# Attention values in batches of eight heads, one transpose for the row maxima, and an earlier place for two batches in a hand-ordered two-layer kernel

## The chip, the cores and the metric

The kernel runs on one core of one Trainium2 chip. The metric is the device time of one execution in microseconds. Three runs of the kernel before took 4024.37, 4029.41 and 4029.52 us; the median is 4029.41 us. A core has five engines that run at the same time: TensorE (PE in the profile; its weight loads are PEld), VectorE (DVE), ScalarE (ACT), GpSimd (POOL) and SyncE (SP), which here issues nearly all DMAs.

## What is computed

The input x is [16, 512, 128] in float32: 16 batches of 512 tokens. Two layers follow, and each adds two branches to its input, both fed with the normalised input.

```
xn = layernorm(x)
x  = x + memory(xn) + block(xn)              # layer 0
xn = layernorm(x)
x  = x + double_attention(xn) + routed(xn)   # layer 1
```

- `memory`: a small two-layer network is trained through 8 chunks of 64 tokens, one after the other (the scan), and then read out for all tokens.
- `block`: a convolution over 3 tokens, attention with 16 heads of 8 channels, a layer norm, and 8 experts of width 512 that all see every token (weighted by a softmax gate).
- `double_attention`: causal attention with 16 heads; its output goes through a convolution and serves as the queries of a second causal attention with the same keys and values.
- `routed`: 32 experts, each token uses 8 of them, and each expert takes at most 128 tokens.

## The kernel before

**A look and a pass of values.** Attention for one batch is split in two halves `c` of 8 heads each. Every half needs two passes over its scores. The first pass, `largest`, I call a look: TensorE makes scores of 128 queries against up to 512 keys for two heads at a time (tile `s`, stationary `q`, moving `k`), and VectorE takes the row maxima into `nm`. The maxima are then negated, split in two parts [...] (`mp`), turned by TensorE into rows (`tpm`), copied by ScalarE (`m`), stored to memory (`topd`) and read back into two spare rows of the query operand `q`, so that the second scores come out with the maximum already subtracted. The second pass, `weighted`, makes the scores the other way round (keys on the partitions), ScalarE takes the exponential into `e`, GpSimd clears what lies above the diagonal (`affine_select`, in layer 1 only), and TensorE multiplies `e` with the padded values `vp`: four heads at a time, each in its own strip of 32 columns of the array, into one PSUM tile `pc`. When all keys are done, `pc` is copied to `cs`, turned back (`tpc`) and divided by the sums.

**Widths.** In layer 0 each pass has 16 tiles of 512 columns with two heads each. In layer 1 the causal mask leaves 512, 384, 256 and 128 columns; `widths` gives 4 tiles of 512 and 4 of 384 with two heads, 2 of 256 with four heads and 1 of 128 with eight: 11 tiles. Layer 0 has 32 looks, layer 1 has 64 (16 batches, two attentions `i`, two halves `c`).

**Turns.** The order of TensorE's work is written out by hand. Each stage is a generator, and `Turns.run` lets every live stage take one step per turn, in the order of priority: looks (0), passes of values (1), and others. One step of `largest` or `weighted` is one tile. Locks make looks follow each other (`p1`), passes of values too (`p2`), and give the PSUM tile `pc` to one pass (`ctx`). Four score slots (`free_slots`) and three tiles of values (`free_values`) are shared by all batches. `room` and `hold` ration three shared PSUM tiles (`work`).

**Filling with experts.** `ffn(b)`, the experts of layer 0, fills what TensorE has left: each turn adds `TURN` = 2750 minus the estimated load of the turn's other matmuls to a credit, and a unit of expert work (`phe` and its ReLU, or `pye`) costs 1000. Where no experts run, `fill` adds matmuls whose result is not used.

**Layer 1.** For batch b, `middle(b)` finishes layer 0, normalises and routes (logits `prl`, counts `pct`, tables `ctab`, `totT`, `xw`); `front1(b)` makes queries, keys and values; `tops` is a look with its loads (`rows_in`); `back` is a pass of values; `between(b)` makes the second queries; `last(b)` ends the batch. Batches start 44 turns apart (`TBB`), which is four looks of 11 turns. After the last `middle`, the pool `mid` closes, `mo` opens in its place, and `moe`, the routed experts, runs with gathers and scatters issued by GpSimd; `total` stores the result.

Of the kernel before, what the change touches and what calls it, by code (L numbers as in the profile page):

```python
# [17 lines left out]
P = 128  # L18
# [64 lines left out]
def network(ctx: ExitStack, tc: tile.TileContext, a, out):  # L83
# [16 lines left out]
        n: [dram.tile([NT8, 2, 32, S], F32, name=f"{n}{i}") for i in range(3)]  # L100
        for n in ("rq0", "rk0", "rq1", "rk1", "r2")
    }
    topd = [dram.tile([16, S], F32, name=f"top{i}") for i in range(4)]
    acc_b = acc[0:N, :].rearrange("(b t p) d -> b p t d", t=TB, p=P)
    xw_b = xw.rearrange("(b t p) d -> b p t d", t=TB, p=P)
    ctab_v = ctab.rearrange("(e i) n -> e i n", i=NTILE)
# [27 lines left out]
        return cols[:, k : k + 1]  # L134

    pools, done, locks, clock, newest, cleared, held, read, cell = {}, {}, set(), [0], [None], [None], [0], [0], []

    def mark(*m):
        done[m] = clock[0]
# [118 lines left out]

    def ends(stage, name):
        yield from stage  # L260
        mark(name)

    def idle(n):
        for _ in range(n):
# [103 lines left out]
    def largest(slot, causal):  # L368


        q, k, at = slot
        yield from acquire("p1")
        nm = att.tile([P, TB, 2, NH], F32, tag="nm", bufs=2, name="nm")
        for i, n, per, t in widths(causal):
            qt = TB - 1 - i
            s = pools["ps"].tile([P, 2, 512], F32, tag="p1", bufs=pools["p1"], name="s1")
            sv = s[:, :, 0 : per * n].rearrange("p r (i n) -> p r i n", i=per)
            for u in range(per):
                for r in range(2):
                    rr = slice(64 * r, 64 * r + 64)  # L380
                    mm(sv[:, r, u, :], q[rr, t + u, qt * P : (qt + 1) * P], k[rr, t + u, :n])
            if causal and per == 1:

                for r in range(2):
                    newest[0] = nc.vector.tensor_tensor_reduce(  # L385
                        out=sv[:, r, 0, :], in0=sv[:, r, 0, :], in1=row["caus"][:, S - n :], scale=1.0, scalar=-BIG,
                        op0=ALU.add, op1=ALU.max, accum_out=nm[:, qt, r, t : t + 1],
                    )
            else:
                if causal:  # L390
                    for r in range(2):
                        dg = sv[:, r, :, n - P : n]
                        nc.vector.tensor_tensor(dg, dg, bc(row["caus"][:, S - P :], 1, per), ALU.add)  # L393
                newest[0] = nc.vector.tensor_reduce(nm[:, qt, :, t : t + per], sv, AX.X, ALU.max)  # L394
            yield
        locks.remove("p1")
        mp = att.tile([P, TB, 2, 2, NH], F32, tag="mp", bufs=2, name="mp")
        nc.vector.tensor_scalar(mp[:, :, :, 0, :].bitcast(FR), nm, -1.0, None, ALU.mult)
        nc.vector.scalar_tensor_tensor(
            mp[:, :, :, 1, :].bitcast(FR), nm, -1.0, mp[:, :, :, 0, :], ALU.mult, ALU.subtract  # L400
        )
        yield
        yield from room()
        tp = work("tpm")[0:16, :]
        for t in range(TB):
            nc.tensor.transpose(tp[:, t * P : (t + 1) * P], mp[:, t].rearrange("p r i x -> p (r i x)"), ident)
        m = att.tile([16, S], FR, tag="m", bufs=1, name="m")
        nc.scalar.copy(m, tp)
        nc.sync.dma_start(at, m.bitcast(F32))
        for r in range(2):  # L410
            nc.sync.dma_start(
                q[64 * r + 32 : 64 * r + 34, :, :].bitcast(F32),
                at[8 * r : 8 * r + 8, :].rearrange("(i t) s -> i t s", t=NH),
            )
        yield

    def weighted(slot, vp, c, causal, cn):
# [4 lines left out]
        old, ends = [], []  # L422
        got = []

        def values(heads):
            for kt, n, t, r, e in heads:
                g = 2 * (t % 2) + r
                j = t // 2
                mm(
                    got[0][32 * g : 32 * g + 32, S - n :], vp[:, kt, 4 * g + 2 * c + j, :], e,  # L430
                    start=(kt == 0 and j == 0), stop=(kt == TB - 1 and j == 1),
                )
            if kt == TB - 1 and t == NH - 1:
                cs = att.tile([P, S], F32, tag="cs", bufs=1, name="cs")
                nc.scalar.copy(cs, got[0])  # L435
                locks.remove("ctx")
                ends.append(cs)

        def tail(n):
            if not got and "ctx" not in locks:  # L440
                locks.add("ctx")
                got.append(pools["ps"].tile([P, 512], F32, tag="ctx", bufs=1, name="pc"))
            for _ in range(n):
                if got and len(old) >= 4:
                    locks.add("values")
                    values([old.pop(0) for _ in range(4)])

        for kt, n, per, t in widths(causal):
# [12 lines left out]
            if causal:  # L461
# [14 lines left out]
        cs = ends[0]  # L476
        yield from room()
        held[0] += 1
        tp = turn4(lambda t: cs[:, t * P : (t + 1) * P], "tpc")
# [138 lines left out]
    pools.update(ps=ps, p1=1, p2=1, work=3, e=3, pairs=True)  # L618
# [18 lines left out]

    fresh = [score_slot(att, i, (nc.gpsimd, nc.vector, nc.gpsimd)[i]) for i in range(3)]
    fresh += [padded_values(att, i) for i in range(2)]
    th = const.tile([P, NT, NC], F32, name="th")  # L640
    gates = const.tile([P, 2, NC], F32, name="gates")
    beta = const.tile([P, NC], F32, name="beta")
# [427 lines left out]
    def back(layer, b, i, c):  # L1070
# [5 lines left out]
        yield from weighted(z[i, c], z["vp"], c, layer == 1, z["cn"])  # L1076
        mark("back", layer, b, i, c)

    def post0(b):
        yield from after(("back", 0, b, 0, 0), ("back", 0, b, 0, 1))  # L1080
# [40 lines left out]
    with tc.tile_pool(name="p0", bufs=1) as p0:  # L1121

        turns.stages += [(t, 2, stage) for t, stage in zip((0, 8, 22, 2, 24), fresh)]
        stage = norm0(p0)
        turns.stages.append((0, 3, ends(stage, "norm0")))
        turns.run(until=lambda: ("norm0",) in done)
    with tc.tile_pool(name="scan", bufs=1) as s1:
        turns.stages.append((turns.turn, 3, ends(scan(s1), "scan")))
        turns.run(until=lambda: ("scan",) in done)


# [11 lines left out]
    def middle(mid, b):  # L1143
# [49 lines left out]
        nc.sync.dma_start(ctab_v[:, b * TB : (b + 1) * TB, :], ct)  # L1193
# [11 lines left out]

    def front1(b):
        yield from after(("x2", b))
        got = []
        yield from take(free_values, got)
        z = live[1, b] = {"vp": got[0]}  # L1210
        xT = l1.tile([P, S], F32, tag="st", bufs=2, name="xT")
        nc.sync.dma_start(xT, xt[1, b])
        yield from idle(2)
        for n, order in (("q", (0, 0, 1, 1)), ("k", (0, 1, 0, 1))):
# [3 lines left out]
            z["r" + n] = rowd[f"r{n}1"][b % 3]  # L1218
            yield from split_rows(pj, col(f"b{n}1"), order, z["r" + n])
        mark("rows", 1, b, 0)  # L1220
        yield from project_values(D1("wv"), row["bv1"], xT, z["vp"])
        mark("vals", 1, b)

# [348 lines left out]
```

## Time and profile before

| | before |
|---|---|
| median of three runs | 4029.41 us |
| the profiled execution | 4017.65 us |
| its span, first to last instruction | 4015.9 us |
| mean granted TensorE clock | 0.964 |
| TensorE busy | 3599.7 us (90%) |
| VectorE, ScalarE, GpSimd busy | 2379.9, 2200.3, 1655.0 us |
| instructions | 62757 |
| DMA | 370.56 MB, 92 GB/s on average |

The profile is of one execution. Groups are named by the tile they write and the tiles they read, as in `pc<-e,vp`. `s<-kx,qx` are the scores of a look, `s<-qx,kx` those of a pass of values. An idle stretch of an engine is put down to what ended it: `PE pc <- POOL e` means that TensorE stood before a value matmul until GpSimd had cleared the mask. In a view in order of time, neighbours of the same kind are merged (`x8`); in a view of stretches each row has the busy time of each engine in one stretch.

### The profile page before, as it was taken

What the parts mean: (1) busy time and instruction counts of PE and PEld (TensorE: products, weight loads), DVE (VectorE), ACT (ScalarE), POOL (GpSimd) and SP (SyncE); (2) the same over time, 40 slices, a digit from 0 to 9 for tenths busy, and PEclk for the clock granted to TensorE, in tenths of its full rate; (3) what the DMA queues carried; (4) which work ended last, traced back from release to release, by engine and by line L of the source; (5) the groups of instructions that cost most, each with busy time, mean ns of one, the idle gap of its engine ahead of it and who ended that gap; (6) DMA issues with size and microseconds to landing.
All of it is one profiled execution on the core that took longest, in us unless ns stands there. A gap on an engine that the chain in (4) does not pass through costs nothing.

```text
span 4015.9 us, 62757 instructions
## 1 busy us (share of the span) xinstructions
PE 3599.7 (90%) x22665; PEld 1942.9 (48%) x22665; DVE 2379.9 (59%) x5203; ACT 2200.3 (55%) x3687; POOL 1655.0 (41%) x2560
## 2 busy tenths in 40 slices
PE   5889989898999889999999999999999999998886
PEld 2445444444544444555555555555555555543343
DVE  5665655665565555564666665656666666567652
ACT  1555655565556776665555555555555555553333
POOL 5433553354334454134333433443333344333664
PEclk7999999999999999999999999999999999998898
DMA  4222222222223333333333333334333333333233
GB/s 155 63 62 71 65 65 71 64 62 62 73 77 93 107 97 104 105 92 123 99 115 102 98 100 109 107 82 117 102 111 91 113 111 89 102 105 83 71 86 85
DMA packets 274199, 370.56 MB, mean 92 GB/s; under 512 B 42168, under 2 KB 123232, under 8 KB 273120
## 3 DMA queue, kind: packets, MB, share of 16 engines
q1 hardware_dynamic: 266720, 359.71, 31.1%
q0 software_dynamic: 7168, 6.82, 1.0%
q8 instruction: 180, 2.95, 0.3%
q14 instruction: 131, 1.07, 0.1%
HBM read 236.59 MB, written 133.25 MB: 92 GB/s over the span
## 4 chain that ended last, share of the span: by engine, by line
PE 64%; DVE 14%; POOL 7%; ACT 5%; issue 5%; DMA 4%; SPq 1%; POOLq 0%; ACTq 0%; DVEq 0%
PE s L190 16%; PE phe L190 10%; PE pye L571 10%; PE pc L190 9%; DVE nm L394 7%; DVE s L393 2%; ACT e L459 2%; PE pgr L190 2%; PE tp L242 1%; DVE s L385 1%; POOL e L463 1%; PE fill L197 1%; PE po L190 1%; PE pq L190 1%; DMA xT<-xt 1%
## 5 line engine op out<-in xcount | busy, mean ns | idle before, releaser
L459 ACT ACTIVATE e<-s 128x1024 f32<-128x1024 f32 (+1 forms) x1216 | 1189.1, 978 | 801.7 <-PE s L190 759.4
L394 DVE TENSOR_REDUCE nm<-s 128x2 f32<-128x1024 f32 (+1 forms) x704 | 861.6, 1224 | 632.1 <-PE s L190 624.9
L385 DVE CUSTOM_DVE_ANT_0 s<-s,sb_const 128x512 f32<-128x512 f32 (+1 forms) x1024 | 647.7, 633 | 644.8 <-PE s L190 626.0
L463 POOL TENSOR_SCALAR_AFFINE_SELECT e<-e 128x128 f32<-128x128 f32 (+2 forms) x1408 | 465.1, 362 | 1133.9 <-ACT e L459 1126.8
L190 PE MATMUL s<-kx,qx 64*128 64x512 f32 (+3 forms) x3072 | 622.7, 431 | 203.4 <-DVE nm L394 106.4
L190 PE MATMUL pc<-e,vp 128*32 128x512 f32 (+3 forms) x6144 | 702.4, 508 | 40.7 <-POOL e L463 39.5
L190 PEld LDWEIGHTS s<-kx,qx 64*128 64x128 f32 x3072 | 276.6, 188 | 778.5 <-issue 317.8
L571 PEld LDWEIGHTS pye<-ew,hTe 128*128 128x128 f32 x4096 | 519.4, 194 | 210.8 <-issue 187.8
L571 PE MATMUL pye<-ew,hTe 128*128 128x128 f32 x4096 | 574.6, 285 | 6.7 <-ACT hT L840 6.5
L190 PE MATMUL phe<-x1T,ew 128*128 128x512 f32 x1024 | 558.0, 630 | 10.3 <-DMA x1T<-x1d 3.9
L190 PE MATMUL s<-qx,kx 64*128 64x512 f32 (+3 forms) x3072 | 532.7, 372 | 26.9 <-ACT e L459 25.8
L563 ACT ACTIVATE hTe<-phe,sb_cols 128x512 f32<-128x512 f32 x512 | 352.9, 689 | 303.9 <-PE phe L190 303.7
L190 PEld LDWEIGHTS s<-qx,kx 64*128 64x128 f32 x3072 | 289.9, 189 | 124.6 <-issue 63.4
L579 POOL TENSOR_TENSOR ac<-ac,y 128x512 f32<-128x512 f32 x128 | 164.8, 1287 | 385.8 <-ACT y L578 367.3
L393 DVE TENSOR_TENSOR s<-s,sb_const 128x256 f32<-128x256 f32 (+1 forms) x384 | 199.5, 519 | 179.5 <-PE s L190 166.4
L190 PEld LDWEIGHTS pc<-e,vp 128*32 128x32 f32 x6144 | 134.2, 109 | 247.7 <-issue 148.4
L190 PEld LDWEIGHTS phe<-x1T,ew 128*128 128x128 f32 x1024 | 159.2, 194 | 123.1 <-issue 87.0
L578 ACT ACTIVATE y<-pye,pr 128x128 f32<-128x128 f32 x512 | 147.1, 368 | 41.8 <-PE pye L571 41.1
L385 DVE DVE_READ_ACCUMULATOR2_ANT nm<- 128x1 f32 x1024 | 144.9, 142 | 0.0
L197 PE MATMUL fill<-sb_pb,sb_const 128*128 128x512 f32 (+3 forms) x252 | 124.8, 583 | 10.5 <-DMA zrow<-zero 10.0
L435 ACT COPY cs<-pc 128x512 f32<-128x512 f32 x96 | 56.3, 586 | 58.4 <-PE pc L190 55.7
L203 POOL TENSOR_SCALAR rs_t<-ss 128x4 f32<-128x4 f32 (+1 forms) x56 | 11.0, 197 | 165.8 <-ACT sq L256 164.0
(294 smaller groups left out, 4031.3 us busy)
## 6 DMA issues: line engine op xcount, KB each, us to landing
ew<-in_ew SPq DMA_DIRECT2D x256, 256.0 KB
kx<-rk SPq DMA_DIRECT2D x192, 256.0 KB
qx<-rq SPq DMA_DIRECT2D x128, 256.0 KB
rq<-hi SPq DMA_DIRECT2D x64, 256.0 KB
rq<-lo SPq DMA_DIRECT2D x64, 256.0 KB
rk<-hi SPq DMA_DIRECT2D x64, 256.0 KB
rk<-lo SPq DMA_DIRECT2D x64, 256.0 KB
qx<-r SPq DMA_DIRECT2D x64, 256.0 KB
```

The lines of the kernel that those rows point to most:

```text
L190: nc.tensor.matmul(o, lhsT=lhsT, rhs=rhs, start=start, stop=stop)
L197: nc.tensor.matmul(o[:, 0:n], lhsT=ident, rhs=cell[0][:, 0:n], start=True, stop=True)
L385: newest[0] = nc.vector.tensor_tensor_reduce(out=sv[:, r, 0, :], in0=sv[:, r, 0, :], in1=row["caus"][:, S - n :], scale=1.0, scalar=-BIG, ...
L393: nc.vector.tensor_tensor(dg, dg, bc(row["caus"][:, S - P :], 1, per), ALU.add)
L394: newest[0] = nc.vector.tensor_reduce(nm[:, qt, :, t : t + per], sv, AX.X, ALU.max)
L435: nc.scalar.copy(cs, got[0])
L459: nc.scalar.activation(e[:, :, 0 : per * n], s[:, :, 0 : per * n], AF.Exp, scale=SCALE)
L463: cleared[0] = nc.gpsimd.affine_select(out=ev[:, r, :, 0:P], in_=ev[:, r, :, 0:P], pattern=[[0, per], [1, P]], compare_op=ALU.is_ge, fill= ...
L563: nc.scalar.activation(hs[i], ph, AF.Relu, bias=col("fb", i))
L571: nc.tensor.matmul(pye[0][:, t, :], lhsT=h[:, t * P : (t + 1) * P], rhs=w2[e][:, f, :], start=(f == 0 and t == 0), stop=(f == 3), skip_gro ...
L578: nc.scalar.mul(y[:, t, :], pye[0][:, t, :], pr[:, t, e : e + 1])
L579: nc.gpsimd.tensor_tensor(ac, ac, y, ALU.add)
```

## The change

Five things are changed.

- **Maxima.** `mp` is now a part of one of two tiles of 128 columns, zeroed once at the start. One transpose of the whole tile takes the place of four of 16 columns; the copy `m` is 64x128 in place of 16x512, and `topd` has that shape, so that both DMAs out of it read rows of 128.
- **Values.** In layer 1, while `mid` is open, values wait until 8 heads are there, and two batches of four then run in the same turn. The `e` tiles come in turn from two pools of three tiles (`att`, `mid`); before there was one ring of three. `lent` holds the heads whose `e` lies in `mid`; `moe` starts once it is empty. After that, batches of four return.
- **Drain.** What is left of a pass of values after its last tile is a stage of its own (`summed`, priority 2), started in the next turn; it may run two batches in one turn.
- **Counts.** `middle` makes the counts of its four token tiles with one matmul in place of four; `ctab` and `totT` are written by four DMAs each, where one DMA and one VectorE copy did it.
- **Order.** `middle` and `front1` start 28 turns sooner for batch 2, 6 for batch 3, 12 for batch 15; the first looks of batch 2 are 20 turns sooner, and the last look of batch 13 is 8 turns later. `front1` takes its tile of values after the rows are made, not first.

```diff
-    topd = [dram.tile([16, S], F32, name=f"top{i}") for i in range(4)]
+    topd = [dram.tile([TB * 16, P], F32, name=f"top{i}") for i in range(4)]
...
-        mp = att.tile([P, TB, 2, 2, NH], F32, tag="mp", bufs=2, name="mp")
+        padded = maxima.pop(0)
+        maxima.append(padded)
+        mp = padded[:, 0 : TB * 16].rearrange("p (t r i x) -> p t r i x", t=TB, r=2, i=2)
...
-        tp = work("tpm")[0:16, :]
-        for t in range(TB):
-            nc.tensor.transpose(tp[:, t * P : (t + 1) * P], mp[:, t].rearrange("p r i x -> p (r i x)"), ident)
-        m = att.tile([16, S], FR, tag="m", bufs=1, name="m")
-        nc.scalar.copy(m, tp)
+        tp = work("tpm")
+        nc.tensor.transpose(tp[:, 0:P], padded, ident)
+        m = att.tile([TB * 16, P], FR, tag="m", bufs=1, name="m")
+        nc.scalar.copy(m, tp[0 : TB * 16, 0:P])
         nc.sync.dma_start(at, m.bitcast(F32))
...
-        def tail(n):
+        def tail(least):
...
-            for _ in range(n):
-                if got and len(old) >= 4:
-                    locks.add("values")
+            if got and len(old) >= least:
+                locks.add("values")
+                for _ in range(min(len(old) // 4, 2)):
                     values([old.pop(0) for _ in range(4)])
...
-            while len(old) >= 4 and not got and "ctx" in locks:
+            while len(old) >= pools["heads"] and not got and "ctx" in locks:
...
-            tail(2)
-            e = att.tile([P, 2, 512], F32, tag="e", bufs=pools["e"], name="e")
+            tail(pools["heads"])
+            pool = pools["weights"][i % len(pools["weights"])]
+            e = pool.tile([P, 2, 512], F32, tag="e", bufs=3, name="e")
...
+                    if pool is not att:
+                        lent.add(id(old[-1]))
...
         free_slots.append(slot)
+        turns.stages.append((turns.turn, 2, ends(summed(old, tail, last, c, cnv), name)))
+
+    def summed(old, tail, last, c, cnv):
         while old:
-            tail(1)
+            tail(4)
             yield
...
-        pct = work("pct")[0:EXP1, :]
+        pct = work("pct")[:, 0:P]
+        mm(pct, lr.rearrange("p t e -> p (t e)"), row["tri"])
+        ct = mid.tile([P, P], F32, tag="st", bufs=4, name="ct")
+        nc.scalar.copy(ct, pct)
         for t in range(TB):
-            mm(pct[:, t * P : (t + 1) * P], lr[:, t, :], row["tri"])
-        ct = mid.tile([EXP1, TB, P], F32, tag="st", bufs=4, name="ct")
-        nc.scalar.copy(ct.rearrange("e t n -> e (t n)"), pct)
-        nc.sync.dma_start(ctab_v[:, b * TB : (b + 1) * TB, :], ct)
+            of = ct[EXP1 * t : EXP1 * (t + 1), :]
+            nc.sync.dma_start(ctab_v[:, b * TB + t, :], of)
+            nc.sync.dma_start(totT[:, b * TB + t : b * TB + t + 1], of[:, P - 1 : P])
...
-        nc.vector.tensor_copy(totT[:, b * TB : (b + 1) * TB], ct[:, :, P - 1])
...
+    ahead = {2: 28, 3: 6, 15: 12}
...
         early = 0 if b < B - 1 else 12 if i else 16 + 8 * c
+        if (b, i) == (2, 0):
+            early = 20
+        if (b, i, c) == (B - 3, 1, 1):
+            early = -8
         return t0 + b * TBB + 20 + 66 * i + 11 * c - early
...
-        [(t0 + b * TBB + 14, 4, front1(b)) for b in range(B)]
+        [(t0 + b * TBB + 14 - ahead.get(b, 0), 4, front1(b)) for b in range(B)]
...
-        turns.stages += [(t0 + b * TBB, 4, middle(mid, b)) for b in range(B)]
+        turns.stages += [(t0 + b * TBB - ahead.get(b, 0), 4, middle(mid, b)) for b in range(B)]
+        pools.update(weights=[att, mid], heads=8)
         turns.run(until=lambda: ("xw", B - 1) in done)
+        pools.update(weights=[att], heads=4)
+        turns.run(until=lambda: not lent)
```

More of the change, by code (lines that the diff above doesn't have):

```diff
@@ L136, in network @@
     pools, done, locks, clock, newest, cleared, held, read, cell = {}, {}, set(), [0], [None], [None], [0], [0], []
+    lent = set()
     def mark(*m):
@@ L260, in ends @@
         yield from stage
-        mark(name)
+        mark(*name)
     def idle(n):
@@ L403, in largest, with weighted @@
         yield from room()
-        tp = work("tpm")[0:16, :]
-        for t in range(TB):
-            nc.tensor.transpose(tp[:, t * P : (t + 1) * P], mp[:, t].rearrange("p r i x -> p (r i x)"), ident)
-        m = att.tile([16, S], FR, tag="m", bufs=1, name="m")
-        nc.scalar.copy(m, tp)
+        tp = work("tpm")
+        nc.tensor.transpose(tp[:, 0:P], padded, ident)
+        m = att.tile([TB * 16, P], FR, tag="m", bufs=1, name="m")
+        nc.scalar.copy(m, tp[0 : TB * 16, 0:P])
         nc.sync.dma_start(at, m.bitcast(F32))
+        at = at.rearrange("(a r i t) s -> r i t a s", r=2, i=2, t=NH)
         for r in range(2):
[L411 to L414, printed above, removed]
+            rows = q[64 * r + 32 : 64 * r + 34, :, :].bitcast(F32)
+            nc.sync.dma_start(rows.rearrange("i t (a s) -> i t a s", s=P), at[r])
         yield
-    def weighted(slot, vp, c, causal, cn):
+    def weighted(slot, vp, c, causal, cn, name):
         q, k, _ = slot
@@ L421, in weighted @@
         cnv = cn.rearrange("p t (a c j d) -> p (t a) c j d", c=2, j=2, d=DH)
-        old, ends = [], []
+        old, last = [], []
         got = []
         def values(heads):
-            for kt, n, t, r, e in heads:
+            for head in heads:
+                kt, n, t, r, e = head
+                lent.discard(id(head))
                 g = 2 * (t % 2) + r
@@ L436, in values @@
                 locks.remove("ctx")
-                ends.append(cs)
-        def tail(n):
+                last.append(cs)
+        def tail(least):
             if not got and "ctx" not in locks:
@@ L442, in tail @@
                 got.append(pools["ps"].tile([P, 512], F32, tag="ctx", bufs=1, name="pc"))
-            for _ in range(n):
-                if got and len(old) >= 4:
-                    locks.add("values")
+            if got and len(old) >= least:
+                locks.add("values")
+                for _ in range(min(len(old) // 4, 2)):
                     values([old.pop(0) for _ in range(4)])
-        for kt, n, per, t in widths(causal):
-            while len(old) >= 4 and not got and "ctx" in locks:
+        for i, (kt, n, per, t) in enumerate(widths(causal)):
+            while len(old) >= pools["heads"] and not got and "ctx" in locks:
                 yield
@@ L472, in weighted @@
         free_slots.append(slot)
+        turns.stages.append((turns.turn, 2, ends(summed(old, tail, last, c, cnv), name)))
+    def summed(old, tail, last, c, cnv):
         while old:
-            tail(1)
+            tail(4)
             yield
-        cs = ends[0]
+        cs, = last
         yield from room()
@@ L617, in network @@
     ps = main.enter_context(tc.tile_pool(name="psum", bufs=1, space=PSUM))
-    pools.update(ps=ps, p1=1, p2=1, work=3, e=3, pairs=True)
+    pools.update(ps=ps, p1=1, p2=1, work=3, weights=[att], heads=4, pairs=True)
     Wt = Pack(load(fa, "pb", [P, sum(PB.values())]), PB)
@@ L639, in network @@
     fresh += [padded_values(att, i) for i in range(2)]
+    maxima = [att.tile([P, P], F32, bufs=1, name=f"mp{i}") for i in range(2)]
+    for t in maxima:
+        nc.gpsimd.memset(t, 0.0)
     th = const.tile([P, NT, NC], F32, name="th")
@@ L1075, in back @@
             z["cn"] = (l1 if layer else fa).tile([P, TB, D], F32, tag="cn", bufs=2, name="cn")
-        yield from weighted(z[i, c], z["vp"], c, layer == 1, z["cn"])
-        mark("back", layer, b, i, c)
+        yield from weighted(z[i, c], z["vp"], c, layer == 1, z["cn"], ("back", layer, b, i, c))
     def post0(b):
@@ L1124, in network @@
         stage = norm0(p0)
-        turns.stages.append((0, 3, ends(stage, "norm0")))
+        turns.stages.append((0, 3, ends(stage, ("norm0",))))
         turns.run(until=lambda: ("norm0",) in done)
     with tc.tile_pool(name="scan", bufs=1) as s1:
-        turns.stages.append((turns.turn, 3, ends(scan(s1), "scan")))
+        turns.stages.append((turns.turn, 3, ends(scan(s1), ("scan",))))
         turns.run(until=lambda: ("scan",) in done)
@@ L1207, in front1 @@
         yield from after(("x2", b))
-        got = []
-        yield from take(free_values, got)
-        z = live[1, b] = {"vp": got[0]}
+        z = live[1, b] = {}
         xT = l1.tile([P, S], F32, tag="st", bufs=2, name="xT")
@@ L1220, in front1 @@
         mark("rows", 1, b, 0)
+        got = []
+        yield from take(free_values, got)
+        z["vp"], = got
         yield from project_values(D1("wv"), row["bv1"], xT, z["vp"])
```

## The prediction

> **What bounds the kernel now.** I read the page's busy shares and its chain of waits first, then busy time by stretch, then the instructions of TensorE in order of time.
>
> ```profile
> PE 3599.7 (90%) x22665; PEld 1942.9 (48%) x22665; DVE 2379.9 (59%) x5203; ACT 2200.3 (55%) x3687; POOL 1655.0 (41%) x2560
> ...
> PE 64%; DVE 14%; POOL 7%; ACT 5%; issue 5%; DMA 4%; SPq 1%; POOLq 0%; ACTq 0%; DVEq 0%
> ```
>
> TensorE is the bound by share and by chain. The stretches (us, then busy us of PE, PEld, DVE, ACT, POOL, granted clock, DMA) show where it is not:
>
> ```profile
> 200.00:1570.00 1370.00, 1226.31 (x7043) 654.73 (x7044) 800.48 (x1035) 840.98 (x1614) 595.80 (x545) 0.96 0.26 74
> 1810.00:3570.00 1760.00, 1640.86 (x11324) 925.54 (x11326) 1068.38 (x2876) 974.64 (x1496) 660.62 (x1423) 0.98 0.36 104
> 3576.00:3675.00 99.00, 86.66 (x586) 40.43 (x580) 70.12 (x193) 44.01 (x54) 37.80 (x92) 0.98 0.31 86
> 3675.00:4016.00 341.00, 263.79 (x1566) 126.99 (x1564) 185.43 (x522) 121.53 (x168) 185.57 (x292) 0.88 0.34 82
> ```
>
> In layer 1 beside the experts of layer 0 (second row) TensorE is busy 93%, so TensorE time saved there is time saved. In the last row, the routed experts beside the last looks, it is 77%: waits count there. TensorE in order of time (start, length, instruction), in the second stretch:
>
> ```profile
> 2326.24 0.60 PE L406 MATMUL tpm<-sb_const,mp 128*16 128x128 f32 x4
> 2326.78 0.50 PE L190 MATMUL s<-kx,qx 64*128 64x512 f32 x2
> 2327.11 0.33 PE L190 MATMUL s<-qx,kx 64*128 64x384 f32 x2
> 2327.37 0.85 PE L190 MATMUL pc<-e,vp 128*32 128x384 f32 x8
> 2328.15 1.12 PE L190 MATMUL phe<-x1T,ew 128*128 128x512 f32 x2
> ```
>
> ```profile
> 2339.05 0.64 PE L190 MATMUL pc<-e,vp 128*32 128x256 f32 x8
> 2339.62 1.16 PE L571 MATMUL pye<-ew,hTe 128*128 128x128 f32 x8
> ...
> 2341.98 0.50 PE L190 MATMUL s<-qx,kx 64*128 64x512 f32 x2
> 2342.42 1.12 PE L190 MATMUL phe<-x1T,ew 128*128 128x512 f32 x2
> ...
> 2344.74 0.43 PE L190 MATMUL pc<-e,vp 128*32 128x128 f32 x8
> 2345.09 0.50 PE L190 MATMUL s<-qx,kx 64*128 64x512 f32 x2
> ...
> 2347.91 0.66 PE L242 MATMUL tpc<-sb_const,cs 128*128 128x128 f32 x4
> 2348.49 0.50 PE L190 MATMUL s<-qx,kx 64*128 64x512 f32 x2
> ```
>
> Take start to next start. Four heads of values (pc, 8 instructions, since each product is done in two passes) take 0.35, 0.57, 0.78 us for 128, 256, 384 columns: 0.215 per 128 columns and a fixed 0.14. A pair of scores of 512 columns takes 0.33 when scores follow (2326.78) and 0.44 when another shape follows (2341.98): a change of shape costs about 0.10. Four transposes of the maxima take 0.54; four of a full 128-column tile 0.58.
>
> VectorE in order of time has one long break between two looks of layer 1:
>
> ```profile
> 1847.73 0.26 DVE L398 TENSOR_SCALAR mp<-nm 128x32 fp32r<-128x32 f32 x1
> ...
> 1879.25 0.70 DVE L385 CUSTOM_DVE_ANT_0 s<-s,sb_const 128x512 f32<-128x512 f32 x1 [12.40 <-PE s L190]
> ```
>
> For 31 us no first pass runs. I counted the rounds ("turns") of the hand-written order and gave each its time by the n-th TensorE instruction: turns 578 to 588 have no first pass, and elsewhere one look (11 turns) follows another; `ffn(15)` ends in turn 1132 (3576 us), the routed experts open in 1170 (3675) and end in 1258 (3977), the last look's output is stored in 1273.
>
> **The change part by part.** The sum stands against the profiled execution, 4017.65 us (span 4015.9 and 1.75 around it); that run lies 11.8 below the median of 4029.41, and I carry the difference over.
>
> *Maxima by one transpose.* Four transposes become one. The further three of four full tiles cost 0.11 each (eight pye in 0.98 give 0.12), so one is 0.58 - 0.33 = 0.25. Saved 0.54 - 0.25 = 0.29 per look, for 96 looks. 54 looks of layer 1 lie in the 93% stretch: 54 x 0.29 x 0.93 = 15. The 32 of layer 0 lie beside the scan, half taken: 5. The last ten: 1. Together -21; bounds -10 and -28. The copy of 16x512 (562 ns) becomes 64x128 (368 ns by the 128-column row y<-pye), on a ScalarE that is 55% busy: nothing. The maxima go through memory as 64 rows of 512 B for 16 of 2 KB, and back as 32 pieces for 8; SP waits some 1.3 us per look for the first landing (86.1 us in 65 waits). A pass of values starts four turns (over 10 us) after its look, which covers it[...]. Two memsets on POOL at the start: hidden.
>
> *Values of 8 heads.* Two batches run back to back, so one fixed part per pair goes. [...] The trace shows the weight loads of one batch:
>
> ```profile
> 2339.05 0.16 PEld L190 LDWEIGHTS pc<-e,vp 128*32 128x32 f32 x8
> ```
>
> All eight loads, those of the second pass too, are done 0.16 us after the batch begins, while its matmuls run 0.64. So loads do overlap on the same rows. I take 0.10 per pair, the shape change above; bounds 0 and 0.14. 54 looks x 4 pairs x 0.10 x 0.93 = -20 ([...]at most -28). Work per turn grows lumpier: sixteen value matmuls of 512 columns take 1.9 us; the experts' credit then gives that turn less. The e ring doubles to six tiles, so exponentials don't wait.
>
> *The drain as its own stage* runs a turn later, behind the next pass's scores, with up to 8 heads. It holds `ctx` one turn longer; the next pass of values asks for it at its fifth tile in layer 1, at its third in layer 0, one turn after it is free: nothing. It relieves TensorE of masks that are not ready:
>
> ```profile
> PE pc L190 <- POOL e L463: 33.0, 24, 4.1
> ```
>
> That is after 3675 us. Of 41 us of such idle time in the whole run 22 are before 128-column batches, the ones drained. I take -12 here and -2 before. Late next are the masks of the other widths.
>
> *Expert counts.* Eight matmuls (1.06 us by the row pct, 16.9 busy over 16) become two of 128 columns, 0.25 by the pye row: 15 x 0.8 x 0.8 = -9. They add seven DMAs per batch. [...] here SP takes 0.45 us and goes on 0.5 us after:
>
> ```profile
> 3671.69 0.45 SPq L1193 DMA_DIRECT2D ctab<-ct  x1
> ```
>
> That is 50 us of a queue that carries 1% of the chain. Only the last batch counts: seven issues before xw, 0 to 3 us, +2 taken. The removed VectorE copy (0.25) is off the path.
>
> *Order.* Batch 2's `middle` and `front1` go 28 turns sooner. Its rows come near turn 568, a slot is free (566), and the look starts at 578, when the first pass falls free: the break closes, and all later looks are 11 turns sooner. Moved with them are some 17 SP issues (about 7 us) and 10 us of POOL work into a busy stretch, past layer 0's last stores and looks' row loads: 0, up to +8. `front1` asking for the value tile after the rows lets the third and fourth batches begin before one is free. But the experts pay: by TURN - load each turn gives them 2750 less some 1365 of attention; one look and one pass of values more before 1132 are some 12300, about nine turns. So `ffn(15)` ends near 1141, at 3.1 us a turn (1855 us over the 598 turns before 1132) +28. `middle(15)`, 12 turns sooner, now follows it at once: xw near 1166, two turns to empty the lent tiles, opening near 1168. 27 turns instead of 38 without experts at 98.3/38 = 2.59: -28. The routed part keeps its 88 turns; the last look then ends some six turns earlier against them, which frees the last store (ao at 4003 us, the scatters land at 3980): -6. Together -6.
>
> Sum: -21 -20 -14 -9 +2 -6 = -68. 4017.65 - 68 = 3950 for the profile, **3961** against the median.
>
> **Rivals.**
> *Layer 1 has another bound (0.22).* Scores have one PSUM buffer per pass; two reductions of 0.70 + 0.14 us and the round trip make a turn over 2 us, near the 2.59 of turns without experts. PE's saving would turn into waiting for nm. For: 36 us of `s <- nm` waits there already. Against: turns there take 3.1. Left: waits -14, order -6, DMAs +2, a quarter of the 50 saved on TensorE: -30, 3999.
> *The experts keep their place (0.18).* If the savings leave `ffn(15)` at 1132 to 1134, the 28 do not appear: -96, 3933. Against: the credit counts its own constants, not time.
> *Slower (0.07).* The burst of sixteen value matmuls delays the next turn's scores, and the experts' units crowd into the other three turns, where PE waits for the ReLU (0.69 us) between phe and pye. One place, 216 bursts: it decides from 68/216 = 0.31 us a burst. At 0.5 us: +108 - 68 = +40, 4069. Against: TensorE idles 10.3 us before phe in the whole run, the largest part, 3.9, for the load of x1T.
> *The look isn't sooner (0.05).* A slot or the rows come late and the break stays; order gives 0 to +8 in place of -6: 3971.
>
> **How the numbers follow.** The main case has 0.48: 3961, its own range 3925 to 3990. The range takes in the second bound and the kept place: 3905 to 4012; about 0.2 is left out, the slower case and parts of the tails. A change under 0.2% (8 us) cannot be told from none. Faster: 0.48 + 0.22 + 0.18 + 0.05, less 0.02 that ends within 8 us: 0.91. Same 0.02, slower 0.07.
>
> **What would show it.** tpm: one instruction of 128 columns per look; x16 pc groups, for 128 columns near 0.6 us instead of two of 0.35; no 31 us break near 1850; pc waits on POOL after the opening below 20 us; the stretch from the last phe (3569) to the first pt (3686) near 87 us, was 117. It is wrong if PE's busy time doesn't fall by about 50 us, or if it falls and waits on nm grow as much.

## The result, and the profile after

| | before | after |
|---|---|---|
| median, us | 4029.47 (4024.37 to 4038.35, 4 runs) | 3962.56 (3959.24 to 3965.53, 4 runs) |
| ratio, 95% interval | | 0.9831, 0.9812 to 0.9851 |
| profiled execution, us | 4017.65 | 3959.24 |
| its span, us | 4015.9 | 3957.5 |
| mean granted clock | 0.964 | 0.952 |

The change saves 67 us; 68 had been forecast. The experiments show that the total is right and its split is not: alone on the kernel before, three of the six terms (maxima, drain, order) are off by 20 us and more, and in the whole the errors cancel.

The first line of the page, busy time by engine:

```profile
PE 3493.7 (88%) x22261; PEld 1922.9 (49%) x22261; DVE 2386.3 (60%) x5187; ACT 2158.8 (55%) x3687; POOL 1654.8 (42%) x2562
```

TensorE works 106 us less, but the kernel ends only 58 us sooner in these two executions, and the granted clock is lower. The stretches (us, then busy us of PE, PEld, DVE, ACT, POOL, granted clock, DMA), cut at the same places of the work as before:

```profile
200.00:1570.00 1370.00, 1205.89 (x6875) 643.34 (x6873) 801.24 (x1023) 824.31 (x1595) 594.90 (x541) 0.96 0.25 73
1810.00:3538.00 1728.00, 1596.97 (x11398) 937.18 (x11398) 1102.57 (x2965) 975.67 (x1538) 666.34 (x1446) 0.97 0.37 109
3538.00:3619.00 81.00, 66.71 (x445) 31.89 (x443) 58.10 (x161) 35.79 (x45) 32.67 (x79) 0.92 0.34 96
3619.00:3958.00 339.00, 267.16 (x1650) 129.68 (x1650) 192.35 (x538) 126.12 (x176) 191.68 (x308) 0.90 0.37 89
```

The third row is the stretch from the end of the experts to the last `xw`, where the routed ones open: 81 us, was 99. TensorE in order of time, in the second stretch:

```profile
2266.92 1.92 PE L192 MATMUL pc<-e,vp 128*32 128x512 f32 x16
2268.78 0.44 PE L192 MATMUL s<-kx,qx 64*128 64x384 f32 x2
...
2277.74 1.50 PE L192 MATMUL pc<-e,vp 128*32 128x384 f32 x16
2279.16 1.16 PE L585 MATMUL pye<-ew,hTe 128*128 128x128 f32 x8
```

Start to next start, a pair of value batches takes 1.86 us at 512 columns and 1.42 at 384. One batch of 384 took 0.78 before: two would be 1.56, so 0.14 per pair is saved. The waits for masks after the opening, and those of the routed part's first matmuls `pt` (us in total, times, longest), were 33.0 us and, for `pt`, this:

```profile
PE pt L190 <- DVE bd L1291: 6.3, 1, 6.3
```

They are now:

```profile
PE pc L192 <- POOL e L471: 23.0, 19, 3.6
PE pt L192 <- DVE bd L1310: 12.7, 2, 12.1
```

A stop of TensorE that the profile of before did not have, in the view in order of time (SyncE's queue, then TensorE; what ended an idle time stands in brackets):

```profile
1803.13 0.38 SPq L1171 DMA_DIRECT2D acc<-x  x1
1803.60 0.46 SPq L1228 DMA_DIRECT2D xT<-xt  x1
...
1806.60 2.08 PE L192 MATMUL pjq<-xT,sb_pd 128*128 128x512 f32 x2 [10.32 <-DMA xT<-xt]
```

`middle(2)`, brought 28 turns forward, stands in SyncE's queue with its store `acc<-x`, which waits 10.4 us for GpSimd to make `x`; behind it is the load of `front1(1)`, and TensorE waits 10.3 us for that. The matmul then runs for 2.08 us where the same one takes 1.10 (at 2573.53 below): the granted clock is 0.5 there, from 1799.7 to 1816.8 us.

### The profile page after: what moved, and what is told of

Same layout as the page of the kernel before. It is cut to its first block, busy times and chain, and to the rows that moved or that the text cites. A ratio compares the mean times of both kernels' runs of the same rounds, so it can differ in the third digit from the quotient of the medians.

```text
span 3957.5 us, 62097 instructions
## 1 busy us (share of the span) xinstructions
PE 3493.7 (88%) x22261; PEld 1922.9 (49%) x22261; DVE 2386.3 (60%) x5187; ACT 2158.8 (55%) x3687; POOL 1654.8 (42%) x2562
## 5 line engine op out<-in xcount | busy, mean ns | idle before, releaser
L192 PE MATMUL s<-kx,qx 64*128 64x512 f32 (+3 forms) x3072 | 630.9, 434 | 258.6 <-DVE nm L396 125.4
L192 PE MATMUL pc<-e,vp 128*32 128x512 f32 (+3 forms) x6144 | 653.6, 513 | 23.7 <-POOL e L471 23.0
L192 PE MATMUL s<-qx,kx 64*128 64x512 f32 (+3 forms) x3072 | 513.1, 357 | 19.0 <-ACT e L467 17.1
L192 PEld LDWEIGHTS pc<-e,vp 128*32 128x32 f32 x6144 | 154.7, 111 | 266.7 <-issue 178.9
L199 PE MATMUL fill<-sb_pb,sb_const 128*128 128x512 f32 (+2 forms) x232 | 116.5, 591 | 9.9 <-DMA zrow<-zero 9.9
```

Of the source, the lines that this page charges most:

```text
L192: nc.tensor.matmul(o, lhsT=lhsT, rhs=rhs, start=start, stop=stop)
L199: nc.tensor.matmul(o[:, 0:n], lhsT=ident, rhs=cell[0][:, 0:n], start=True, stop=True)
```

## The experiments

Saved time is (1 - ratio) x 4029, so that kernels measured at different times can be set side by side; each ratio's interval is 0.0017 to 0.0027 either way, 7 to 11 us.

### The parts alone, and eights taken away

`e1` is the kernel before with the maxima part only; `e2` with the drain only; `e3` with the order only (`ahead`, the two shifts of looks, and the values tile taken after the rows). `e4` is the kernel after with

```diff
-        pools.update(weights=[att, mid], heads=8)
```

In `e2` (and in `g2` below, other than its expectation says) the second attention of batch 13 in layer 1 works on data that are not its own; the instructions are the same. Its place is near turn 1222, behind the stretch in which the gain of these two kernels will be found.

> The kernel before with one part of the change alone: one transpose of a padded 128-column tile for the maxima, the 64x128 copy and the turned store. Theory (the time goes with TensorE's work): the changed kernel's trace has one such transpose at 0.20 us where four took 0.53, so 96 x 0.33 = 32 us less TensorE work, about 25 us of time: 4004. Rival (TensorE's saving turns into waits for the maxima in layer 0 and for VectorE in layer 1): under 10 us, 4020 or more.

> The kernel before with the drain alone: the last heads of a pass of values are a stage of its own (priority 2), one turn later, up to two batches per turn; values stay at four heads. Theory: TensorE's waits for masks after the opening of the routed experts fall by half, 10 to 15 us: 4015 to 4020. Rival (the changed kernel stands 20 us behind at the end of the scan because the drain falls in a turn that the experts of layer 0 wanted): layer 0 loses what the end gains, 4029 or more, with the end of the scan some 15 us later than the kernel before has it.

> The kernel before with the order alone: middle and front1 of batches 2, 3 and 15 sooner, the first looks of batch 2 sooner, the last look of batch 13 later, the value tile taken after the rows. Theory: the 31 us break near 1850 us closes, the experts pay with nine turns, and the stretch without experts gets shorter: -6, 4023. Rival A (the loads of the batches brought forward stand in SP's queue behind waits and stop TensorE): the 10 us stop before pjq appears here as well, and the time is 4029 to 4040. Rival B (the experts do not pay): 3995 to 4005.

> The changed kernel with values of four heads throughout and one ring of three e tiles. Theory: the fixed 0.138 us per pair comes back, 54 x 4 x 0.138 = 30 us of TensorE work, some 25 us of time: 3988. Rival (the pairs gain more, because the exponentials had to wait for a free e tile or because fewer waits for masks are left): 4000 or more. Rival (the pairs are hidden): under 3970.

| | median, us | ratio, interval | saved |
|---|---|---|---|
| e1 maxima | 4033.53 | 1.0006, 0.9981 to 1.0031 | -2 |
| e2 drain | 3959.87 | 0.9843, 0.9825 to 0.9861 | 63 |
| e3 order | 3979.12 | 0.9895, 0.9877 to 0.9913 | 42 |
| e4 after, fours | 3986.70 | 0.9914, 0.9891 to 0.9937 | 35 (after: 68) |

Eights are worth 24 us by the medians, 33 by the ratios (about 12 either way): the term of 20 stands, nearer to its bound of 28. `e4` also goes back to one ring of three `e` tiles; ScalarE's waits for a free tile (`e` behind `pc`, 1570 to 3640 us) are then 6.2 us, with two rings 0.8, so the second ring can be a small part of this gain. The other terms do not stand. The maxima, 21 us in the sum, give nothing; drain and order, 20 together, give 105, more than all parts together do.

**Where the maxima's time went.** TensorE in order of time around the queries of one batch, first before, then e1:

```profile
2571.69 1.08 PE L190 MATMUL prl<-sb_pd,xT 128*128 128x32 f32 x8
2573.53 1.10 PE L190 MATMUL pjq<-xT,sb_pd 128*128 128x512 f32 x2 [0.77 <-DMA xT<-xt]
```

```profile
2571.82 0.27 PE L407 MATMUL tpm<-sb_const,mp 128*128 128x128 f32 x1
2572.02 0.51 PE L190 MATMUL s<-kx,qx 64*128 64x512 f32 x2
...
2578.93 1.08 PE L190 MATMUL prl<-sb_pd,xT 128*128 128x32 f32 x8
2581.94 2.05 PE L190 MATMUL pjq<-xT,sb_pd 128*128 128x512 f32 x2 [1.93 <-DMA xT<-xt]
```

The transpose takes 0.20 us start to start, which saves the 0.33 that e1's expectation names (the prediction had 0.25 and 0.29). But `pjq` now waits 1.93 us for its operand, was 0.77, and runs twice as long. SyncE's queue shows why, again before and e1:

```profile
2567.24 0.88 SPq L411 DMA_DIRECT2D qx<-top  x2
2568.41 0.35 SPq L1164 DMA_DIRECT2D xt<-xT  x1
...
2570.50 0.32 SPq L1212 DMA_DIRECT2D xT<-xt  x1
```

```profile
2574.74 1.65 SPq L414 DMA_DIRECT2D qx<-top  x2
2576.51 0.35 SPq L1168 DMA_DIRECT2D xt<-xT  x1
...
2578.72 0.32 SPq L1216 DMA_DIRECT2D xT<-xt  x1
```

Over all 192 of them, issuing a `qx<-top` takes SyncE 0.62 us where it took 0.25 (medians; the transfer has 32 pieces for 8), and `top<-m` 0.50 for 0.34: 0.90 us per look. `front1`'s store and load of the turned tile stand behind, and TensorE behind the load, in 13 batches:

```profile
PE pjq L190 <- DMA xT<-xt: 9.9, 13, 1.7
```

```profile
PE pjq L190 <- DMA xT<-xt: 21.3, 13, 2.4
```

(waits from 1570 to 3640 us: sum, number, longest; before and e1). That is 11 of the missing 21 to 28 us. The clock can account for the rest, by the estimate below.

**The clock.** The record of the granted clock has two values, 1 and 0.5, and every change lies on a grid of 3.413 us, in all 14 traces of this study. For e1, four steps of the grid, the third beginning just before the `pjq` above:

```profile
2575.00:2578.41 3.41, 3.41 (x25) 2.07 (x28) 1.90 (x5) 3.07 (x8) 0.99 (x3) 1.00 0.30 96
2578.41:2581.82 3.41, 1.60 (x16) 0.97 (x8) 1.68 (x5) 0.96 (x2) 1.61 (x3) 1.00 0.47 147
2581.83:2585.24 3.41, 3.30 (x12) 1.52 (x16) 0.58 (x2) 0.77 (x2) 0.00 (x0) 0.50 0.00 0
2585.24:2588.65 3.41, 3.13 (x29) 1.53 (x22) 3.38 (x21) 1.97 (x2) 1.28 (x3) 1.00 0.72 269
```

In the second TensorE is busy 1.60 of 3.41 us; the next runs at half clock. Counted from 1600 to 3540 us over the 14 traces, steps at full clock:

| TensorE busy in the step | steps | next one at half clock |
|---|---|---|
| under 0.5 | 81 | 80 |
| 0.5 to 0.6 | 150 | 73 |
| 0.6 to 0.7 | 256 | 17 |
| over 0.7 | 7174 | 9 |

Of the steps at half clock that were over 0.9 busy, 175 of 216 had full clock behind them; of those under 0.8 busy, none of 56. The wait of 1.93 us before `pjq` lies, but for its last 0.1 us, in e1's step of 1.60. Not every such wait has half clock behind it: eight of e1's 13 waits for `xT` have, one of 2.06 us has not, and in before two of 1.7 us have not; what makes the difference was not shown. I estimate that one step at half clock costs up to 1.7 us of TensorE, half of the 3.41 us, since `pjq` takes 2.05 us in such a step and 1.10 at full clock. Between 1570 and 3640 us before has 19 such steps, e1 38; 17 to 20 of e1's (by how near counts), and none of before's, have a `pjq` that waited for `xT` just ahead. By that estimate the difference is at most 19 x 1.7 = 32 us, beside the 11 of waiting: enough to take all that the transposes save. The expectations below call a step a window, and their clock theory is this count with that estimate: fewer steps under 0.6 busy, fewer windows at half clock, some 1.7 us each. The spread of one kernel's runs goes with the clock as well: of ten runs of before, 4016.13 us had clock 0.964 and 4034.78 us had 0.955, some 2.1 us for each 0.001. After has 45 such steps (the 49 of an expectation below counts a stretch whole that runs past 3640 us).

### Without front1's load

If this is right, the maxima must show their value where no `pjq` can wait for that load. In `f1` to `g4` `front1` uses the tile that `middle` has turned:

```diff
-        xT = mid.tile([P, S], F32, tag="st", bufs=4, name="xT2")
+        xT = x2T[b] = l1.tile([P, S], F32, tag="x2T", bufs=1, name="xT2")
         transpose_tokens(xT, xn2)
-        nc.sync.dma_start(xt[1, b], xT)
...
-        xT = l1.tile([P, S], F32, tag="st", bufs=2, name="xT")
-        nc.sync.dma_start(xT, xt[1, b])
+        xT = x2T[b]
```

`middle` turns it only after the values of the batch before are made, and for room the ring `gt` of `moe` has 10 or 11 tiles in place of 12; in the kernels made from after, the ring `st` of `mid` has 3 in place of 4. The experts and `xw` keep their turns (`ffn(15)` ends in 1132 in f1 as in before, in 1126 in f3 as in after).

> The kernel before, but front1 multiplies the tile that middle has turned (kept in layer 1's pool) and neither stores nor loads xT; the order of turns is the same. It is the control for f2. Clock theory: [...] In the profile of before 10 us of waits pjq <- xT lie in 13 places, each 0.8 us[...]: they go, 8 us, 4016; half-clock windows between 1570 and 3640 us stay near 19. Rival (these waits are taken up by the next wait): 4024.

> The maxima part alone, and front1 without its load as in f1. Clock theory: in e1 these waits had grown to 1.6 us and 17 of 38 half-clock windows of 1570 to 3640 us stood right behind one of them. Without the load they cannot come: 20 to 24 windows, and the maxima show their TensorE time: 15 to 21 us under f1, near 3998. Rival (the transposes were never on the path): within 5 us of f1, and the windows don't matter.

> The kernel after, and front1 without its load. 19.5 us of waits pjq <- xT in four places go (10.3 us of them where a store waits ahead of the load on SP), and with them some 11 half-clock windows of 1.7 us: clock theory 3963 - 19 - 19 = 3925, some 37 windows between 1570 and 3640 us for 49. Rival (the next load is late in its place): 3950 to 3963.

> f3, and the matmuls without use (fill) begin in the first turn without expert work where they began in the third. Most windows under 0.6 busy in layer 1 lie where one batch of experts ends and the next begins. Clock theory: windows between 1850 and 3520 us fall from 26 to about 10, 27 us: near 3900. Rival (the added matmuls hold up the scores of those turns): as slow as f3 or up to 15 us slower, with the windows fewer.

| | median, us | ratio, interval | saved | half-clock steps, 1570 to 3640 us |
|---|---|---|---|---|
| f1 before, no load | 3996.97 | 0.9927, 0.9911 to 0.9944 | 29 | 15 |
| f2 maxima, no load | 3971.24 | 0.9857, 0.9835 to 0.9878 | 58 | 16 |
| f3 after, no load | 3945.09 | 0.9789, 0.9771 to 0.9807 | 85 | 40 |
| f4 f3 and sooner fill | 3939.67 | 0.9778, 0.9757 to 0.9798 | 89 | 35 |

f2 against f1: the maxima save 29 us (26 by the medians), where alone they gave nothing, with as many half-clock steps. So it was the load, with what follows from it, that hid their value; how much of that was waiting and how much clock, f2 does not separate. f1 itself saves 29 where I expected 8; the waits are 9.9 and the steps 4, and some 12 us of it I cannot place. f3 gains 17 us on after, about its 19.5 us of waits for `xT`; the steps fell by 5 only, where some 11 were expected, and waits for the maxima of the masked tiles (`nm`, line 387) grew from 39.1 to 47.6 us. f4 has fewer steps between 1850 and 3520 us, but 18 for 24 where 10 were expected, and its time is not told apart from f3's: it decides nothing.

### Drain and order on that base

> The order part alone, and front1 without its load: to be set against f1 (3997). e3 (order alone) gained 45 where the prediction had 6; its experts end in turn 1138, near the 1141 of the prediction, but a turn between the experts' fifth and fifteenth batch took 3.02 us instead of 3.13. Theory A (this was waiting for xT and the clock behind it: 13 waits became 4, 18 half-clock windows 6): without the load most of it is gone, some 10 are left: 3987. Theory B (looks and passes of values now meet at other tiles, so that TensorE waits less for the maxima nm in each turn): 25 to 35 are left: 3962 to 3972.

> The drain part alone, and front1 without its load; the tile that front1 reads is not in the ring of cT, xo and xs here, so that the data of every batch is its own. Against f1 (3997). The prediction's own step: -14, 3983. Theory A (e2's gain was the wait for xT and the clock): 3975 to 3985. Theory B (e2's busy time per turn fell because two left-over batches run together, and not between the next pass's scores): layer 1 gains 40 to 50, the scan's stretch loses 20 to 30 as in e2: 3960 to 3975.

> f3 (the kernel after, front1 without its load: 3945) without the order part. By the prediction's step, order is worth 6: 3951. If it is worth in company what it was alone in e3: 3985. If drain and order give the same thing twice (fewer waits and switches in the turns of layer 1): 3945 to 3955, with the break of 31 us open again.

> f3, and in layer 0 the drain runs in place, ahead of the next work, as it does in the kernel before; in layer 1 it stays a stage of its own. In the two kernels with the drain stage the scan ended 20 to 30 us later in the same turn (1593 and 1602 us against 1572). If the stage is the cause: the scan ends near 1573, and the kernel comes to 3925 to 3932. Rival (the turns that layer 0 loses are made up by the experts of layer 0, which come 8 to 12 turns sooner with the stage): 3940 to 3950.

`g1` and `g2` are f1 with the part; `g3` is f3 with `ahead = {}` and without the two shifts of looks; `g4` is f3 with

```diff
-        turns.stages.append((turns.turn, 2, ends(summed(old, tail, last, c, cnv), name)))
+        stage = ends(summed(old, tail, last, c, cnv), name)
+        if causal:
+            turns.stages.append((turns.turn, 2, stage))
+        else:
+            yield from stage
```

Below are the medians, and the stages of the profiled execution in us, cut by turns as in the prediction: end of the scan; from there to the end of `ffn(5)`; the ten batches of experts to `ffn(15)` with the mean turn; to the last `xw`; to the last batch's output.

| | median, us | ratio, interval | saved | scan | to ffn(5) | to ffn(15), per turn | to xw | to the end |
|---|---|---|---|---|---|---|---|---|
| before | 4029.47 | | | 1572 | 374 | 1630, 3.13 | 98 | 325 |
| f1 | 3996.97 | 0.9927 | 29 | 1570 | 371 | 1610, 3.09 | 96 | 321 |
| g1 order | 3966.55 | 0.9846, 0.9819 to 0.9872 | 62 | 1572 | 401 | 1575, 3.02 | 68 | 330 |
| g2 drain | 3953.39 | 0.9822, 0.9797 to 0.9847 | 72 | 1597 | 357 | 1562, 3.02 | 108 | 316 |
| f3 | 3945.09 | 0.9789 | 85 | 1589 | 387 | 1539, 2.98 | 82 | 334 |
| g3 no order | 3918.19 | 0.9729, 0.9704 to 0.9754 | 109 | 1586 | 360 | 1521, 2.94 | 115 | 314 |
| g4 | 3888.79 | 0.9662, 0.9638 to 0.9686 | 136 | 1576 | 399 | 1512, 2.92 | 66 | 323 |

*Drain.* On f1 it saves 43 us, theory B's size. In the stretch of the ten batches TensorE has 10512 and 10460 instructions in f1 and g2, and works 52 us less:

```profile
1941.00:3551.00 1610.00, 1511.16 (x10512) 852.13 (x10508) 997.18 (x2698) 903.07 (x1381) 611.45 (x1324) 0.99 0.35 101
```

```profile
1954.00:3516.00 1562.00, 1459.25 (x10460) 836.95 (x10460) 998.83 (x2677) 893.23 (x1375) 607.53 (x1316) 0.99 0.36 104
```

The left-over heads run together behind the next pass's scores and no longer between them. In this stretch two neighbouring matmuls of TensorE differ in the part of the array that they use (as `64*128` and `128*32`) 1615 times in f1 and 1419 times in g2. At the 0.10 to 0.14 us that a change of shape and the fixed part of a batch take, that is 20 to 27 of the 52 us; 4 half-clock steps fewer (14, now 10) are, at the estimated 1.7 us each, up to 7 more. Some 20 us have no cause shown. In layer 0 the same stage costs time: the scan ends 27 us later in g2. There a first pass of scores waits more for the maxima (waits of TensorE from 200 to 1569 us, for f1, f3 and g4; g2 alone has 66.9 us in 55 waits):

```profile
PE s L190 <- DVE nm L394: 41.3, 36, 6.3
```

```profile
PE s L192 <- DVE nm L396: 68.5, 56, 3.9
```

```profile
PE s L192 <- DVE nm L396: 44.4, 39, 6.3
```

With the drain in place in layer 0 (g4) the waits go back, the scan ends 13 us sooner than in f3, and the kernel is 51 us faster, not 13 to 20. The other gains stand in the later columns, with 11 half-clock steps for 24 between 1850 and 3520 us. With the stage in place the experts of layer 0 keep their turns (`ffn(2)` in 431, for 419), so they meet the looks at other tiles; that this is the cause is likely, not shown.

*Order.* In g1 the prediction's two large terms can be read: to `ffn(5)` 30 us more (28 forecast for the experts' nine turns), and 28 less to `xw` (28 forecast). What it did not have is the middle column, 35 us less. There the end of a look (its maxima stored) and the end of a pass of values (its sums taken) lie 3 turns apart before (the look later) and 1 turn apart with the order part (the pass later). The half-clock steps fall from 14 to 6, and TensorE has fewer waits that are put down to "issue", that is to nothing that the profile shows (f1, then g1, with g1's row for the stretch):

```profile
PE s L190 <- issue: 24.4, 22, 1.6
```

```profile
PE s L190 <- issue: 8.3, 7, 2.0
1973.00:3548.00 1575.00, 1498.39 (x10528) 844.83 (x10526) 999.93 (x2688) 899.79 (x1381) 612.00 (x1319) 0.99 0.36 103
```

Against f1's row above TensorE is idle 22 us less and busy 13 us less for as many instructions, which the 8 half-clock steps fewer (up to 14 us, by the estimate of 1.7 each) can cover. With the new drain (f3 against g3) the same shift makes that column 18 us longer, not shorter, and the order part costs 24 us in all.

## Why the prediction was right or wrong

- *TensorE is the bound of layer 1, and time saved on it is saved.* Half right. Where TensorE works less and its waits do not grow, the time is saved (f2 against f1, and the stretch of ten batches in g2). But 93% busy hides steps of 3.4 us that are under 0.6 busy, and of 231 such steps, counted above, 153 had half clock behind them.
- *Maxima, -21.* The price on TensorE was right (0.33 a look for 0.29; 29 us in f2). The step that failed is "SP waits some 1.3 us per look for the first landing ... A pass of values starts four turns (over 10 us) after its look, which covers it". The landing was covered: no wait of TensorE for `qx<-top` shows in e1 between 1570 and 3640 us. The time to issue the two reads, 0.37 us more each, was not looked at, nor who stands behind them in the queue: `front1`'s load, then TensorE. That step was costed at nothing; it shows as 11 us of waits, with an estimated 32 at most of half clock beside them, and together they can take all that the part saves.
- *Eights, -20.* Right: 24 to 33 us. The reading of the trace held (eight weight loads done in 0.16 us while their matmuls ran 0.64); a pair saves 0.14 us, the upper bound that I had, not 0.10.
- *Drain, -14.* Mis-sized. The waits for masks after the opening fell by 10 us in the whole change, forecast 12. The term "-2 before" is the one that failed: I counted waits there and not the changes of shape, though 0.10 us for each stood in the prediction. It is 48 us in the stretch of the ten batches (20 to 27 of TensorE's 52 us there are changes of shape, see above), less 27 that layer 0 loses; "at its third in layer 0 ... nothing" was wrong too.
- *Counts, -9 and +2.* Not run alone, so both stay open. In after the last batch's `totT` rows are issued from 3617 to 3625 us among other transfers, and the routed part's first matmul waits 12.1 us, where it waited 6.3. But the added DMAs are not shown to be the cause: `e2`, which has none of them, waits 11.2 us at this place, and `g4`, which has them all, 2.7. From the issue of the last `xw` to that matmul it is 7.9 us in before, 8.0 in e2, 8.2 in g4 and 10.2 in after, which fits the +2.
- *Order, -6.* The -28 was right in size and cause: in g1 it is -28, and from the last `phe` to the first `pt` it is 88 us for the 87 that were forecast. The +28 (g1: +30) was right in size by luck: the experts reach `ffn(5)` 5 turns later and not nine, some 15 us, and the rest is that a turn takes 3.02 us there for 2.90 in f1. The -6 at the end has the wrong sign: in g1 the last look ends 2 turns later than before (turn 1253 for 1251), not sooner, and that column is 9 us longer. In the whole change, too: before, the last `fin<-acc` and the last `ao<-xo` were issued at 4002.79 and 4003.34 us; after, at 3939.04 and 3945.96: the looks came 7 turns sooner and the opening 11, so the last look is now what is late. The moved DMAs, "0, up to +8", are the stop of 10.3 us. And the shift of looks against passes was not seen at all: the stretch of ten batches is 35 us shorter with it in g1 and 18 longer in f3.
- *The experts end in turn 1141.* It was 1138 with the order part alone (g1), and 1126 in the kernel after, as if they had kept their place. The drain stage had brought them 12 turns forward in layer 0 (`ffn(2)` in turn 419 for 431), while the scan ended 21 us later.
- *The rivals.* The bursts cost nothing that shows: pairs gain (e4). The break did close. That the experts keep their place came in turns (they end in 1126), but the -96 that was to follow from it did not. That layer 1 has another bound is partly so: of 106 us that TensorE no longer works, 58 reached the end of the profiled execution.
- *What would show it.* One `tpm`, pairs of values (two batches of 128 columns in 0.57 us for the 0.6 forecast), no break near 1850 us and PE's fall of over 50 us came as said. The waits for masks are 23.0 us, not below 20. From the last `phe` to the first `pt` it is 105 us, not 87: 30 turns from `ffn(15)` to `xw` and not the 26 of g1, and a first matmul that waits 12 us for 6. The waits of the looks' scores for `nm` grew, in the whole run, from 106 to 125 us, less than PE's time fell; the growth is in layer 0, where the drain brings it (41.4 to 65.3 us).

So the total came out right by luck: the waits, the clock, layer 0 and the shifted order took back what the drain and the pairs gave above their terms. The parts don't add: on the base without the load they save 29 (maxima), 33 (order) and 43 (drain), which is 105, and with the eights and counts on top only 56 come out.

g4 is the fastest kernel of the study: 3888.79 us (3884.76 to 3904.20, 6 runs), 0.9662 of before with its interval below that of after. Whether it gains further without the order part was not run.

## What to carry to other kernels

Cost a changed DMA by the time its queue takes to issue it (here 0.62 us where it was 0.25) and by what stands behind it in that queue, and follow that to the engine that is the bound. The TensorE of before is 90% busy on average and yet has a mean granted clock of 0.964: look for steps of 3.4 us under 0.6 busy (153 of 231 had half clock behind them here), and count a wait in one of them at its own length and, by the estimate above, up to 1.7 us for each step at half clock behind it. A gain that a part shows only in some company may be hidden or made by such waits; measure a part on a base from which the wait is gone.

## What was not expected of the hardware

- Of the steps of 3.413 us at full clock, 80 of 81 in which TensorE was under 0.5 busy had half clock behind them, and 9 of 7174 that were over 0.7 busy; of those at half clock and over 0.9 busy, 175 of 216 had full clock behind them.
- Issuing a read of 16 KB took SyncE's queue 0.62 us in 32 pieces (e1, after) and 0.25 us in 8 (before).
- Two value batches back to back took 1.86, 1.42, 1.00 and 0.57 us at 512, 384, 256 and 128 columns in after, where one took 1.00, 0.78, 0.57 and 0.35 in before: 0.13 to 0.14 us saved, the whole fixed part of one batch, at each of the four widths.
